# The same steps of seven interleaved lanes in other orders: a two-layer graph-attention and feed-forward kernel

## The chip, the cores and the metric

The kernel runs on one core of one Trainium2 chip. The time is device microseconds of one launch, from its first to its last instruction and what the runtime adds; lower is better. In the text PE is the matmul engine (PEld its weight loads), DVE the vector engine, ACT the scalar engine, POOL the GpSimd engine and SP the engine that issues most DMAs.

## The reference

The input is x, 64 batches of 256 tokens with 256 numbers each, in float32, and an adjacency matrix of 256 x 256. Two layers follow each other; every stage starts with a layer norm and is added to x.

```python
x = x + gnn0(layernorm(x), adj)     # mlp1, attention over all tokens, mlp2, attention over adj
x = x + ffn0(layernorm(x))          # the top half of the tokens by a score goes through gelu MLP
x = x + gnn1(layernorm(x), adj)     # one attention layer over adj
x = x + ffn1(layernorm(x))          # Mamba-2 block: conv, 8 heads of decays, gated norm, projection
```

ffn0 has to know the rank of every token within its batch (a token's score against all 256), gathers the upper half in the order of rank, and scatters the result back. Batches are independent of each other.

## The kernel before, in words

Two batches form a group of 4 x 128 tokens, so there are 32 groups (numbered 0 to 31). Each group passes through four pieces of code, and each piece is a Python generator: it issues some instructions and yields. A piece in progress is called a lane, and it has a letter:

| letter | what it runs | steps in a group |
|---|---|---|
| a | gnn0 of a group (group 0 in two halves: a and d) | 55 (half: 42) |
| g | ranks of the tokens, scatter to DRAM, fetch of the upper half (`ranked_tokens`) | 9 |
| b | ffn0 without the ranks, and gnn1 | 50 |
| c | ffn1 (the last group in two halves: e and f) | 87 (half: 78) |
| w | weights made ready | 13, once |

Three strings say in which order the lanes take their steps. Each letter runs one step of its lane. FIRST (310 letters) starts the kernel. Then ORDER (201 letters) is repeated 29 times; each pass takes one whole group's worth of steps of every one of a, b, c and g, but of different groups: when a pass starts, a is about to begin group k, g group k-1, b has done 23 steps of k-2 and c 7 steps of k-3. An upper-case letter in ORDER allows a lane to begin its next group. LAST (407 letters) ends it. There is no scheduler beside this: the order in which instructions are issued is the order in which they stand in each engine's own queue, and an engine never overtakes in its queue. So a letter's place decides, on each of the five queues, what stands ahead of its instructions. Semaphores between engines follow from the data and the buffers.

In the text a step is named by lane and number: c8 is the eighth step of lane c. These are the steps that matter here, with the lines of the profile (all matmuls go through the helper `mm`, L239, and all transposes through `tr`, L242, so PE's rows are told apart by their tiles):

- a3: xn, the layer norm (DVE, L395). a4, a5: its transposes pt (PE), copied to xT by ACT (L409). a10 to a13, a18 to a21: matmuls pp with W_fc. a14: fb (PE), most and top (DVE, L427, L428). a15 to a17: e and its sums on DVE and ACT, then e is scaled on POOL (L470). a22, a23: transposes pt of e (PE), copied by ACT (L486). a24, a27, a30, a33: matmuls u, each followed by two exponentials on ACT (L493, L496) with DVE between and after (L495, L498), and an add on POOL (L567). a36, a37: mlp2. a38 to a41: matmuls with W_hand. a42 to a47: the second attention; a48, a51: u again. a54, a55: transposes pr, and DVE's L595 and L596.
- g2, g3: xn and score (DVE, L395, L604, L607). g5: wrow, the score along a row (PE). g6, g7: ranks (DVE, L623, L626), `to` and `back` (L632, L633). g8: four indirect DMAs from POOL that write `sorted` to DRAM (L637). g9: two DMAs on SP that fetch `taken` (L643).
- b2: psel, the transposes of `taken` (PE), copied to sel by ACT (L657). b3, b8, b13, b18: matmuls ph; after each come ACT (L673, L678), POOL (L679), DVE (L681), ACT (L682) and DVE (L684), which makes g. b23 to b30: py with g. b31: y (DVE) and its DMA to DRAM. b32: gather by POOL (L709). b33, b34: L716 on DVE, L719 on POOL, statistics L383. b39: fb. b42: e on POOL; b43, b44: its transposes. b45 to b49: pa and u. b50: statistics for c.
- c3: xn. c4, c5: transposes of xn, xT; c5 also has pd, the matmul for dt. c6: L787, L789 on DVE, Exp and Ln on ACT (L790, L791). c7: L793, L794 and the scan csT (L795) on DVE. c8: pn, transposes of dtT and csT. c10 to c30: five convolutions, each pp on PE, L857 on ACT, three L861 on DVE, Tanh on ACT (L866), L867 on DVE, with the decays E on POOL (L835) and ACT (L842) between. c33, c35, c37, c39: transposes of xs. c43, c44, c53, c54, c63, c64, c69, c70: E times cb (DVE, L915). c45, c55, c65, c71: pz; c47, c57, c67, c73: py with E; then DVE's L940 and POOL's L941. c75 to c79: the norm. c80 to c86: po.

The step function and its loops:

```python
    with tc.manual_schedule():
        for lane in FIRST:
            step(lane, True)
        while at["a"] < n:
            for letter in ORDER:
                step(letter.lower(), letter.isupper())
        for lane in LAST:
            step(lane, True)
```

Of the kernel before, what the change touches and what calls it, by code (L numbers as in the profile page):

```python
# [19 lines left out]
GELU_C = 0.7978845608028654  # L20
GELU_A = 0.044715
FIRST = (
    "dwadadaddwadwaaaaddddddadaadaddaawaaadaddadaaddaddaadaaaadadaddaawadaadadaddawddcadadaacaaadaddadaaa"
    "gwaawgggggagaaaagaawaaagaaaaaababbababagaaaaabbbbabbabbababaabababwwbaaaabababaaaabaaabbbbbabbbabaga"
    "gagbababaababbaaaaabaaggabgabbggaaabaaabagabcbbabababbbacabbaabbbbbabaaccaabcbaacawaabwbbaacbcababaa"
    "babaabgabb"
)
ORDER = (
    "cbAbcccaaccbbbbcbabacccccacccccaaaccbcbccaaaabacbcbabaaaaccbacaabcabccbccbccacaccaaGcbbaacacccbcbgcg"
    "ccacgaaacggabccccccgcccgcgbacbccccccaccbcaacBabacaabcaccbaccbbbbbcabccbccbCaaacaabacccbbacbacbbbbabb"  # L30
    "b"
)
LAST = (
    "cfefbcfcfcbfbeeefgcfeccbfcbbffebecececbcccccegeccefccbfcefebecfbcfccccccebcefbccfcebccccfcfcbccbecff"
    "bfeccbcfeccfbegffccecbbccebcceeececeececfcccbcgecffebfffeebfcfccccegfffcbccgefbgccbffbcebbfecfccbcfc"
    "cbbegffbcecbccbcgcebbefcccfcfbefccfcecbebcecececfebecfcecbfccegcfbbbcccfbecbcecbcceecfccfcefceeccfec"
    "febfebffbeccefbcbecbecfbcfebcfeccfffbcefccbbccccbfbccfbbeccbfccbcbcecefcfbceccccccccbcbfeebcbcbcbfec"
    "bcbccec"
)


# [1061 lines left out]
```

## Time and profile before

| what | value |
|---|---|
| median of 3 runs | 3633.09 us (3630.11 to 3633.62) |
| the profiled execution, its own time | 3634.4 us |
| its span in the profile | 3632.7 us |
| FIRST, by the trace | 0 to 217.0 us |
| 29 passes of ORDER | 217.0 to 3362.6 us |
| LAST | 3362.6 to 3632.7 us |
| mean granted clock of PE | 0.987 |

The bounds of the parts are the starts of the first matmuls of each part. In the profile's rows, a group is named by line, engine, operation and tiles (out<-in), with its count; "idle before" is the time that the engine stood still ahead of it, with the engine or DMA whose signal ended that. In an answer on waits the columns are the total of us, the number of times and the longest. In a row of the timeline the first two numbers are start and length in us, "xN" the number of merged instructions, and in brackets the idle time before it and what ended it. A matmul of float32 has two records in the trace, a transpose one; matmuls overlap, so their lengths add up to more than the time that they take. The runs shown lie within 0.1% of each other; the profiled execution is 1.3 us above their median.

### The profile page before, as it was taken

The numbers are of one execution on the slowest core, as the hardware profiler recorded it, in microseconds if no ns is written. First come the engines' busy times: TensorE is split into PE (matmuls) and PEld (weight loads), VectorE is DVE, ScalarE is ACT, GpSimd is POOL, SyncE is SP. The second block draws the span as 40 slices with busy tenths as digits, with TensorE's granted clock in tenths as the row PEclk, the third lists the DMA queues.
The fourth block names the chain that finished last, engine by engine and source line by source line (L and its number), as shares of the span: only waits on it lengthen the run. The fifth ranks groups of instructions, "written<-read, shape, count | busy, mean of one in ns | idle before, by whom it ended". The sixth has DMA issues, their size and how long they took to land.

```text
span 3632.7 us, 51434 instructions
## 1 busy us (share of the span) xinstructions
PE 3461.4 (95%) x16236; PEld 2445.3 (67%) x16236; DVE 2803.0 (77%) x7142; ACT 2190.2 (60%) x5166; POOL 1599.5 (44%) x2040
## 2 busy tenths in 40 slices
PE   8999999999999999999999999999999999999675
PEld 6666676676676676676676677676677676677444
DVE  5577778877788877788877787877787887787765
ACT  4466666666666666666666666666666666666443
POOL 2334444444445444444444444434444444444432
PEclk9999999999999999999999999999999999999887
DMA  3012101111201211201111211111211111211111
GB/s 116 25 45 65 62 28 60 60 63 57 65 29 57 63 60 57 66 32 52 63 60 58 66 39 50 62 57 58 66 52 38 60 58 58 66 51 34 59 53 43
DMA packets 120992, 201.29 MB, mean 55 GB/s; under 512 B 18448, under 2 KB 79760, under 8 KB 120720
## 3 DMA queue, kind: packets, MB, share of 16 engines
q1 hardware_dynamic: 108432, 164.44, 14.0%
q0 software_dynamic: 12288, 33.57, 3.0%
q8 instruction: 129, 2.11, 0.2%
q14 instruction: 143, 1.17, 0.1%
HBM read 151.03 MB, written 42.73 MB: 53 GB/s over the span
## 4 chain that ended last, share of the span: by engine, by line
PE 47%; DVE 28%; ACT 14%; POOL 5%; issue 4%; DMA 1%; SPq 0%; ACTq 0%; DVEq 0%; POOLq 0%
PE pp L239 9%; DVE xs L861 9%; PE u L239 9%; PE po L239 6%; PE py L239 5%; PE pz L239 4%; PE ph L239 4%; ACT E L842 4%; POOL e L470 3%; PE pa L239 3%; PE pt L242 3%; DVE xn L395 3%; DVE junk L729 2%; DVE st L383 2%; ACT xs L857 2%
## 5 line engine op out<-in xcount | busy, mean ns | idle before, releaser
L239 PE MATMUL pp<-W_fc,o 128*128 128x256 f32 (+1 forms) x2048 | 459.9, 379 | 0.2 <-DVE W_fc L274 0.2
L842 ACT ACTIVATE E<-E,ncs 128x256 f32<-128x256 f32 (+1 forms) x1024 | 376.8, 442 | 131.0 <-POOL E L835 131.0
L861 DVE SCALAR_TENSOR_TENSOR xs<-pp,conv_w,xs 128x510 f32<-128x510 f32 (+5 forms) x495 | 360.8, 730 | 121.5 <-ACT xs L857 92.0
L239 PEld LDWEIGHTS pp<-W_fc,o 128*128 128x128 f32 x2048 | 383.3, 190 | 67.4 <-issue 12.8
L470 POOL TENSOR_SCALAR e<-e,den 128x256 f32<-128x256 f32 x384 | 225.4, 604 | 351.8 <-DVE den L467 171.5
L239 PE MATMUL pp<-xT,W_in 128*128 128x512 f32 (+1 forms) x660 | 298.8, 586 | 0.0
L567 POOL TENSOR_TENSOR o<-w,o 128x512 f32<-128x512 f32 (+1 forms) x132 | 170.4, 1293 | 241.6 <-DVE w L498 241.6
L835 POOL TENSOR_SCALAR_AFFINE_SELECT E<-E 128x256 f32<-128x256 f32 x512 | 225.4, 470 | 104.2 <-DMA E<-csd 102.7
L915 DVE TENSOR_TENSOR E<-E,cb 128x768 f32<-128x768 f32 (+1 forms) x264 | 254.7, 996 | 0.0
L239 PE MATMUL pz<-xT,W_in 128*128 128x512 f32 (+1 forms) x528 | 248.8, 595 | 0.0
L239 PE MATMUL py<-w,g 128*128 128x256 f32 x1024 | 243.4, 385 | 5.6 <-DVE g L684 3.5
L383 DVE BATCH_NORM_STATS2 st<-xt 128x6 f32<-128x256 f32 x512 | 185.3, 414 | 79.9 <-POOL xt L764 52.4
L239 PE MATMUL ph<-sel,w 128*128 128x256 f32 x1024 | 242.5, 380 | 0.7 <-ACT sel L657 0.7
L239 PE MATMUL u<-at,h 128*128 128x256 f32 x1024 | 241.1, 384 | 0.2 <-ACT at L486 0.2
L239 PE MATMUL pp<-o,mlp_w 128*128 128x512 f32 (+1 forms) x528 | 231.2, 580 | 2.3 <-POOL o L567 2.2
L239 PE MATMUL po<-W_ol,xs 128*128 128x256 f32 x1024 | 232.7, 381 | 0.0
L239 PE MATMUL pp<-xT,mlp_w 128*128 128x512 f32 (+1 forms) x528 | 231.9, 583 | 0.2 <-ACT xT L409 0.2
L496 ACT ACTIVATE w<-w,neg 128x512 f32<-128x512 f32 (+1 forms) x196 | 139.9, 714 | 152.2 <-DVE w L495 152.1
L679 POOL TENSOR_SCALAR g<-g 128x512 f32<-128x512 f32 x128 | 91.5, 715 | 316.8 <-ACT g L678 312.0
L395 DVE TENSOR_SCALAR xn<-xt,mv,rstd 128x256 f32<-128x256 f32 x512 | 222.7, 491 | 5.6 <-POOL rstd L255 4.9
L866 ACT ACTIVATE th<-xs 128x512 f32<-128x512 f32 (+1 forms) x165 | 102.1, 619 | 207.2 <-DVE xs L861 202.9
L239 PEld LDWEIGHTS py<-w,g 128*128 128x128 f32 x1024 | 187.0, 190 | 55.3 <-DVE g L684 30.0
(174 smaller groups left out, 7906.2 us busy)
## 6 DMA issues: line engine op xcount, KB each, us to landing
E<-csd SPq DMA_DIRECT2D x248, 384.0 KB
xt<-in_x_dram SPq DMA_DIRECT2D x31, 512.0 KB
out_dram<-xt SPq DMA_DIRECT2D x31, 512.0 KB
taken<-sorted SPq DMA_DIRECT2D x64, 128.0 KB
ranked<-y SPq DMA_DIRECT2D x64, 128.0 KB
cs<-xs SPq DMA_DIRECT2D x64, 64.0 KB
E<-csd SPq DMA_DIRECT2D x16, 192.0 KB
w<-in_L_ffn_w_dram SPq DMA_DIRECT2D x2, 1024.0 KB
```

The lines of the kernel that those rows point to most:

```text
L239: nc.tensor.matmul(to, lhsT, rhs, start=start, stop=stop)
L242: nc.tensor.transpose(to, of, eye)
L383: nc.vector.bn_stats(st[:, c, :], xt[:, c, :])
L395: nc.vector.tensor_scalar(chunk(xn, c), xt[:, c, :], mv[:, c, 0:1], rstd[:, c : c + 1], ALU.subtract, ALU.mult)
L470: nc.gpsimd.tensor_scalar(e, e, den[:, c : c + 1], 1.0, ALU.mult, ALU.mult)
L496: nc.scalar.activation(w, w, AF.Exp, bias=neg1)
L567: nc.gpsimd.tensor_tensor(o1[m], w, o1[m], ALU.add)
L835: nc.gpsimd.affine_select(out=diag[:, b], in_=diag[:, b], compare_op=ALU.is_ge, fill=-3e38, base=0, pattern=[[0, 2], [1, P]], channel_mult ...
L842: nc.scalar.activation(e[:, b, to], e[:, b, to], AF.Exp, bias=ncs[:, b, half, h : h + 1])
L861: nc.vector.scalar_tensor_tensor(s3[:, :, d:], p3[:, :, : N - d], conv_w[:, m, 3 - d : 4 - d], s3[:, :, d:], ALU.mult, ALU.add)
L866: nc.scalar.activation(th, s, AF.Tanh)
L915: nc.vector.tensor_tensor(e2, e2, cb2, ALU.mult)
```

## The change

The three strings are replaced by others. Each has as many letters as before, and as many of each letter, and after FIRST and after every pass each lane stands at the same step as before. No instruction is added, removed or altered; what differs is their order in the engines' queues, and with it which buffers are in use at a time. The words given with it: "Other orders of the lanes' steps, searched in a model with longer hand-overs between engines; nothing else differs". In FIRST 85% of the letters' steps stand at another place (by 4.6 places on average), in ORDER 76% (2.4; at most 12), in LAST 97% (10.4; the steps of g up to 101 places earlier).

```diff
 FIRST = (
-    "dwadadaddwadwaaaaddddddadaadaddaawaaadaddadaaddaddaadaaaadadaddaawadaadadaddawddcadadaacaaadaddadaaa"
-    "gwaawgggggagaaaagaawaaagaaaaaababbababagaaaaabbbbabbabbababaabababwwbaaaabababaaaabaaabbbbbabbbabaga"
-    "gagbababaababbaaaaabaaggabgabbggaaabaaabagabcbbabababbbacabbaabbbbbabaaccaabcbaacawaabwbbaacbcababaa"
-    "babaabgabb"
+    "dwaaddaaddddaadwaadddadaaacdaadaadwacdwdaaaddddaadadaaaaadadddaddaaadadaaddaddadwadaadaaaadddadaagcg"
+    "aaagwgaggaagaaagaaaaawaawgaaabaabaaaaaabbaabgabbawbbbaaaabaabwbaabbabaaabbabbabababaagbabbbbabbabaaa"
+    "agagaaabagabbbbababaaaaabbaaaggbabaaabbgagagawbbaabbabaaagbbcacbacbbbaacabaabbbbabbbawcbbccaabbbaaba"
+    "baawbaaabb"
 )
 ORDER = (
-    "cbAbcccaaccbbbbcbabacccccacccccaaaccbcbccaaaabacbcbabaaaaccbacaabcabccbccbccacaccaaGcbbaacacccbcbgcg"
-    "ccacgaaacggabccccccgcccgcgbacbccccccaccbcaacBabacaabcaccbaccbbbbbcabccbccbCaaacaabacccbbacbacbbbbabb"
-    "b"
+    "bAcbcccaaccbbbcbaacbccbccacccccaaacccbbccbacaaaabbaacbcccaccbaacaaabacbabaccccbcGaaaccacabbccacaacbb"
+    "gccaccgcbagcccgacgbgcccccgaccccccagbcccccaacbBabacbbaccabaccbcccbcbbabcbcCacbbcbbacaaacabcabbbacbabb"
+    "b"
 )
 LAST = (
-    "cfefbcfcfcbfbeeefgcfeccbfcbbffebecececbcccccegeccefccbfcefebecfbcfccccccebcefbccfcebccccfcfcbccbecff"
-    "bfeccbcfeccfbegffccecbbccebcceeececeececfcccbcgecffebfffeebfcfccccegfffcbccgefbgccbffbcebbfecfccbcfc"
-    "cbbegffbcecbccbcgcebbefcccfcfbefccfcecbebcecececfebecfcecbfccegcfbbbcccfbecbcecbcceecfccfcefceeccfec"
-    "febfebffbeccefbcbecbecfbcfebcfeccfffbcefccbbccccbfbccfbbeccbfccbcbcecefcfbceccccccccbcbfeebcbcbcbfec"
-    "bcbccec"
+    "fcccbceececccbfeeefbbbccfbebfgfcgcbfeecegecefgbfcfccecfcfebecbcccffccbcccbfcccfcefbfcfcffccccefbcccc"
+    "ccbcfefcfcfccegbecccfbcceccgccbeggccecceefceffcbcefcbbegceeceebcfbbefcebeccbfccecfccbefecbcccfecebfb"
+    "cffcfcbcbfecebbccfbbbccbfecccfcbffcceceebcbebcceccecceceeefccecbcccbbcffceccgeccecbeebecceebfbebfccf"
+    "fffcfcbfebfecfcebbcbefbccbcccccbfebfffcfcfcecbcccccbbbfffbbecbccbfcfbceccebccccfbbfcefeebbbcbfcefceb"
+    "ccccefc"
 )
```

A letter whose lane cannot begin yet does nothing: so it is for 3 of c and 2 of g in FIRST, before and after, and in LAST for nearly all of e and f (and before for 10 of b). What is then left is taken in turns, a step of each lane that is left, after the string is over: before, b of the last group from step 41, c from step 85, and e and f; after, c from step 85, and e and f. In the new ORDER c8 and b25 open the pass instead of b25 and c9; c33 stands behind a14; c5 directly behind a51; b24 ahead of the next pass's c8; g5 to g8 about c57 to c65.

## The prediction

> **What bounds the kernel now.** I read the page first, then busy time by stage, then the waits of PE, then the order of time at the places where PE waits.
>
> ```profile
> span 3632.7 us, 51434 instructions
> PE 3461.4 (95%) x16236; PEld 2445.3 (67%) x16236; DVE 2803.0 (77%) x7142; ACT 2190.2 (60%) x5166; POOL 1599.5 (44%) x2040
> PEclk9999999999999999999999999999999999999887
> ```
>
> PE is the busiest engine, and its clock is whole except in the last three slices. The windows of the three parts of the schedule (FIRST, the 29 passes of ORDER, LAST; after the width come the busy times of PE, PEld, DVE, ACT and POOL with their instructions, the clock, the DMA share and GB/s):
>
> ```profile
> 0.00:217.00 217.00, 193.88 (x836) 144.63 (x836) 119.58 (x407) 111.41 (x279) 68.34 (x97) 0.98 0.19 60
> 217.00:3362.60 3145.60, 3086.40 (x14618) 2181.00 (x14618) 2505.67 (x6346) 1968.11 (x4641) 1441.23 (x1825) 1.00 0.17 55
> 3362.60:3632.70 270.10, 181.10 (x784) 119.71 (x784) 177.76 (x391) 110.65 (x249) 89.97 (x118) 0.83 0.16 52
> ```
>
> The passes hold 87% of the time, 3145.6 / 29 = 108.5 us each, and PE (first number after the width) is busy in 98% of it: any order can win back only PE's waits there. In LAST PE is idle for 89 us, but that part waits on a chain through DVE and ACT. Who PE waits for, over the whole run:
>
> ```profile
> PE pt L242 <- DVE xs L867: 40.8, 9, 7.0
> PE pt L242 <- POOL e L470: 22.3, 61, 2.7
> PE pn L242 <- DVE csT L795: 21.7, 31, 0.8
> PE pn L242 <- DVE dtT L793: 14.0, 31, 1.9
> PE pd L239 <- ACT xT L409: 7.2, 30, 0.2
> PE psel L242 <- DMA taken<-sorted: 6.7, 4, 3.3
> ```
>
> The first row (9 times) is LAST. The rows with some 30 or 60 times come in every pass. They undercount, since a matmul's end is modelled: from one matmul's start to the next, less its own length at the pace of its row, I get 3.1 us of true waiting in a pass (pn 1.4, pt of e 1.1, pd 0.4, py 0.2). That is the most the new ORDER can gain: 29 x 3.1 = 90 us.
>
> **The change, part by part.** Nothing is added or removed; 76% of ORDER's letters stand elsewhere, by 2.4 places on average. So I take each place where PE waits, or nearly waits, and compare the matmuls that cover the wait with the chain that has to end in it. Starts of matmuls are 0.216 us apart for 256 columns, 0.43 for 512, 0.109 for a transpose, and a pass takes about 4% more than their sum.
>
> *1. The ranks (g5 to b2).* The chain today:
>
> ```profile
> 1906.88 0.60 PE L242 MATMUL wrow<-ident,wc 128*128 128x128 f32 x4
> 1914.32 0.45 DVE L632 CAST to<-rank 128x4 uint32<-128x4 f32 x1
> 1915.28 1.63 POOL L637 DMA_INDIRECT sorted<-xn,to  x1 [0.18 <-issue]
> 1922.59 0.97 POOL L637 DMA_INDIRECT sorted<-xn,to  x1 [1.72 <-DMA sorted<-xn,to]
> 1921.07 4.45 SPq L643 DMA_DIRECT2D taken<-sorted  x2
> DMA to landing us min/median/max: 2.4/2.5/3.7
> 1928.64 0.60 PE L242 MATMUL psel<-ident,taken 128*128 128x128 f32 x4
> ```
>
> From the end of `to` (1914.8) to the landing of `taken` is 0.5 + 8.3 of POOL + 1.6 to the second issue on SP (0.32 long, over at 1925.5) + 2.5 = 12.9 us, all latency that no order shortens. PE asks for it 13.8 us after `to`: under 1 us to spare, and 4 passes already waited. In the new order the work of PE between wrow and psel falls from 20.1 us to 17.95 (a36 and c65 and much else change sides), by today's ratio (21.3 real) to 19.0. DVE needs after wrow: about 1.1 until gz and xs of c56 and c58 are out of its way, then g6 2.0, b48 1.1, g7 2.6, in all 7.0. So PE arrives 12.0 us after `to`: a wait of 0.9 to 1.2 us. I take **+1.2**, as POOL also has c59, b48 and c61 ahead of the scatter.
>
> *2. pd (c5).* Each pass xT's copy ends just before pd. In the new order a51's matmuls stand directly before c5, so on ACT the exponential of a51 (0.60 us) stands ahead of that copy and cannot start until a51 ends. The wait goes from 0.4 to about 0.05 + 0.3 + 0.6 + 0.6 - 0.43 = 1.2: **+0.8**. Behind that copy on ACT stand a52, b16 and c6.
>
> *3. pn (c8).*
>
> ```profile
> 1949.80 1.11 PE L239 MATMUL pd<-xT,W_dt 128*32 128x256 f32 x8 [0.24 <-ACT xT L409]
> 1954.90 0.31 PE L242 MATMUL pn<-ident,dtT 64*128 64x64 f32 x2 [0.37 <-DVE dtT L793]
> 1955.90 0.33 PE L242 MATMUL pn<-ident,csT 64*128 64x64 f32 x2 [0.70 <-DVE csT L795]
> 1956.17 1.13 PE L239 MATMUL py<-w,g 128*128 128x256 f32 x4
> ```
>
> From the end of pd to csT is 4.9 us. The new order puts b24's py (0.85) ahead of pn: the cover goes from 3.4 to 4.3. But a54's two operations on DVE (0.68 + 0.69) now follow b18 on PE and stand straight before c7; they push csT to 5.2. Net **-0.4**.
>
> *4. xs's transposes (c33).* They go from after a18 and a19 (3.4 us of matmul) to directly behind fb of a14, and need L867 of c30. On DVE that now stands behind b34, whose statistics wait for POOL's add:
>
> ```profile
> 1876.41 0.74 DVE L383 BATCH_NORM_STATS2 st<-xt 128x6 f32<-128x256 f32 x2
> 1877.88 0.75 DVE L383 BATCH_NORM_STATS2 st<-xt 128x6 f32<-128x256 f32 x2 [0.72 <-POOL xt L719]
> 1878.55 0.36 DVE L385 BATCH_NORM_AGGREGATE mv<-st 128x2 f32<-128x6 f32 x4
> ```
>
> b34 ends at 1878.9, L867 takes 0.69: 1879.6, and PE would be at c33 at 1878.1 to 1878.6. **+1.0**. In return c35 and c33 are out of the way of a22, whose e (L470) waits for the same DVE queue: the two waits of a22 and a23 nearly go, **-0.9**.
>
> *5. Smaller ones.* a4 comes one py (0.88) earlier against xn of a3, which had 0.95 to spare with DVE 0.4 sooner: +0.5. b26 meets g of b22 half a microsecond sooner: +0.3. c4 waits for c3, now behind b11 and b12 on DVE: +0.3. The next pass's b13 and b18, po (c80 to c86), pa and the E products of c63, c64, c69, c70 keep 0.5 us or more and are costed at nothing; if DVE runs a microsecond late, py of c47, c57 and c67 is late next.
>
> *6. Credit.* While PE waits, DVE, ACT and POOL go on, so a later wait is shorter: -0.7, an estimate: a quarter of the sum of items 1 to 5 (1.2 + 0.8 - 0.4 + 1.0 - 0.9 + 1.1 = 2.8). I round the remainder to **+2.0 us a pass**, 58 us in 29.
>
> *The clock.* Windows with the same columns:
>
> ```profile
> 123.00:126.40 3.40, 1.71 (x9) 1.00 (x10) 0.57 (x2) 1.30 (x5) 1.86 (x4) 0.99 0.02 5
> 126.40:129.80 3.40, 3.40 (x10) 2.69 (x9) 0.69 (x1) 1.11 (x2) 0.62 (x1) 0.50 0.00 0
> ```
>
> PE was idle for half of one stretch (one wait, 2.9 us), and the next ran at 0.50. The Trainium skill ("TensorE: Matmul & The Clock Gate", Part 1: The HAM clock gate) asks for at least one idle window of about 3.4 us before the clock halves; by it my waits would never cost more than themselves. The row says less is enough. Waits up to 1.9 us left the clock whole (psel's of 1.1 us at 1601, 224.6 with 1.9). By page and row alike the sum stays at +58 with waits of 1.2; but by the row a psel wait of 2.5 us would add half of 3.4, 1.7 us a pass, 49 us.
>
> *FIRST and LAST.* FIRST: the 2.9 us wait for e at 124 and the two around 45 keep their neighbours; 0, between -5 and +5. LAST: the last group's ranks (g) come up to 101 places sooner. Today PE waits 2.30 + 3.26 us there for `taken`, and then runs at half clock for a while. The wait goes; c30 starts some 5 us sooner and b31's `y` some 9 sooner, of which DVE takes back 3 to 6, since b33 now stands on DVE ahead of c56 and waits through the gather with nothing beside it. The tail of e and f, taken in turns, stays. **-6**, between -12 and +8.
>
> *Sum.* 3634.4 (the profiled execution's own time; span 3632.7) + 58 - 6 = 3686. The median shown is 1.3 lower, so 3685.
>
> **The rivals.**
> - *Faster.* If item 1 does not bite, because DVE reaches g7 a microsecond sooner (b48 or c58 in its shadow), and c30's L867 is out before fb, then what is left is what the new order covers better: pn (4.3 instead of 3.4), a22, a51. Waits would fall from 3.1 to some 1.5 us a pass: -46 - 6, 3582; half of it gives 3608. It decides where `to` ends: 13 us before psel. For it: three of the five repeated waits get more cover. Against: the hand-overs in these rows are 0.05 to 0.1 us, so an order chosen for long ones buys cover that this chip does not need.
> - *No change.* Gains and losses in a pass cancel, and LAST gives its 6: 3628. The letters are locally permuted, and PE is busy 98%; but that needs a cancellation within 0.25 us a pass.
> - *Much slower.* The wait for `taken` passes 2.5 us and the clock halves once a pass: 3685 + 38 (a further 1.3 us a pass) or more, 3723 to 3740. For it: POOL's queue ahead of the scatter; against: c61 is ready early.
> - *That it does not do what it says*: each string keeps its count of each letter, so after FIRST and every pass each lane stands at the same step; the change is order alone.
>
> **How the numbers follow.** Some 0.2% (7 us) is what a measurement of this kernel can tell. Slower as worked out, 3650 to 3723: 0.59. Much slower: 0.15. Within 7 us: 0.06. Faster: 0.20. Predicted 3685. The range goes down to 3605, which leaves about 0.12 of the faster case out, and up to 3740 with 0.06 beyond.
>
> **What would show it.** Right: a pass of about 110.5 instead of 108.5; PE's wait of psel for `taken` in most passes, some 1 us each; pd's idle up from 0.24; pt of xs (L867) waiting in every pass; pn's wait for dtT gone. Wrong: psel without waits, or a pass under 108.5. If the clock shows 0.5 inside the passes, the third rival is at work.

## The result, and the profile after

| | before | after |
|---|---|---|
| median | 3632.89 us (3630.11 to 3633.62, 4 runs) | 3712.95 us (3709.76 to 3719.19, 4 runs) |
| profiled execution, its own time | 3634.4 us | 3710.0 us |
| FIRST | 217.0 us | 217.3 us |
| 29 passes of ORDER | 3145.6 us (108.5 each) | 3221.3 us (111.1 each) |
| LAST | 270.1 us | 269.7 us |

The changed kernel is slower: ratio 1.0224, 95% interval 1.0206 to 1.0242, so 80 us. The three parts of the schedule, as busy time by stage with the columns of before:

```profile
0.00:217.30 217.30, 192.90 (x836) 144.94 (x837) 121.12 (x407) 112.44 (x281) 68.12 (x98) 0.98 0.21 63
217.30:3438.60 3221.30, 3123.32 (x14618) 2204.31 (x14617) 2547.78 (x6347) 1964.78 (x4641) 1477.66 (x1826) 0.99 0.17 54
3438.60:3708.30 269.70, 178.26 (x784) 119.25 (x784) 171.75 (x390) 107.47 (x244) 87.40 (x117) 0.82 0.16 52
```

Of the 75.6 us between the two profiled executions the passes hold 75.7, FIRST 0.3 and LAST -0.4. Two things in the row of the passes are odd for a mere change of order: DVE is busy 42 us longer (2547.78 against 2505.67) and PE 37 us, with the same instructions, and PE's clock is 0.99 instead of 1.00. Waits of PE over the whole run:

```profile
PE pt L242 <- DVE xs L867: 59.6, 38, 8.9
PE pd L239 <- ACT xT L409: 55.3, 31, 1.8
PE pn L242 <- DVE csT L795: 20.1, 32, 0.8
PE pt L242 <- POOL e L470: 7.6, 5, 2.9
PE pn L242 <- DVE dtT L793: 6.9, 4, 2.2
PE psel L242 <- DMA taken<-sorted: 2.2, 3, 1.2
```

pd's wait for xT has grown from 7.2 to 55.3 us, once in every pass. This is the place in the order of time; the first pd in the list is k = 0, the second has to wait for the second copy of xT:

```profile
1091.60 0.60 ACT L493 ACTIVATE w<-u 128x512 f32<-128x512 f32 x1 [0.23 <-PE u L239]
1092.16 2.35 POOL L770 TENSOR_TENSOR xt<-xt,b_lin 128x1024 f32<-128x1024 f32 x1
1092.23 2.56 DVE L495 TENSOR_SCALAR w<-w 128x512 f32<-128x512 f32 x1 [1.12 <-ACT w L493]
1094.10 0.62 PE L239 MATMUL pd<-xT,W_dt 128*32 128x256 f32 x4
1094.83 0.72 ACT L496 ACTIVATE w<-w,neg 128x512 f32<-128x512 f32 x1 [2.15 <-DVE w L495]
1095.46 0.58 ACT L493 ACTIVATE w<-u 128x512 f32<-128x512 f32 x1
1095.93 0.58 ACT L409 COPY xT<-pt 128x512 f32<-128x512 f32 x1
1096.56 0.63 PE L239 MATMUL pd<-xT,W_dt 128*32 128x256 f32 x4 [1.84 <-ACT xT L409]
1097.12 3.05 PE L239 MATMUL ph<-sel,w 128*128 128x256 f32 x8
```

L495, a minimum over 128x512 that takes 0.42 us elsewhere, takes 2.56 us here. It starts 0.07 us after POOL's L770, the add of b_lin in c5, and ends 0.28 us after that add ends. ACT's L496 waits for it (2.15 us), the next exponential and the copy of xT stand behind L496, and PE at pd. In the kernel before the same add begins beside other operations:

```profile
1948.78 2.36 POOL L770 TENSOR_TENSOR xt<-xt,b_lin 128x1024 f32<-128x1024 f32 x1 [5.73 <-DVE xn L395]
1948.84 0.69 DVE L498 SCALAR_TENSOR_TENSOR w<-w,u 128x512 f32<-128x512 f32 x1
1950.96 0.48 DVE L787 TENSOR_SCALAR dtT<-pd,dtb 64x256 f32<-64x256 f32 x1 [1.43 <-PE pd L239]
```

L498 runs within the add and is not longer for it. So theory A is: L495 stands still while the add runs, and that is the whole loss. Its rival (B) is the prediction's own account of pd, the exponential of a51 ahead of the copy on ACT.

The last line of the fence of the kernel after shows a second effect: eight matmuls ph took 3.05 us instead of some 1.9. The clock halves. Four stretches of 3.41 us, in two pairs that follow each other (after the width PE, PEld, DVE, ACT and POOL, then the clock, the DMA share and GB/s):

```profile
1094.46:1097.88 3.42, 1.58 (x12) 0.83 (x9) 2.57 (x6) 2.92 (x5) 0.05 (x1) 1.00 0.00 0
1097.88:1101.29 3.41, 3.41 (x13) 2.85 (x12) 1.71 (x4) 2.97 (x7) 0.00 (x0) 0.50 0.02 5
```

```profile
1207.10:1210.52 3.42, 1.80 (x10) 1.26 (x11) 2.71 (x6) 2.97 (x6) 0.00 (x0) 1.00 0.02 5
1210.52:1213.93 3.41, 3.41 (x22) 2.80 (x20) 3.08 (x7) 3.29 (x6) 0.00 (x0) 1.00 0.00 0
```

The same wait at pd lies in both pairs. Where PE was busy 1.58 us of the stretch, the next ran at 0.50; where it was busy 1.80, nothing happened. (Experiment 5 shows that this share alone does not decide it.) All the stretches of half clock in the passes begin on one grid of 3.413 us, and 14 of the 29 passes have one, as a rule where the wait falls into a single stretch of the grid. From one wrow to the next (28 of these, which leave out the ends), passes without one take 110.04 us on average and passes with one 112.15.

### The profile page after: what moved, and what is told of

Same layout as the page of the kernel before. It is cut to its first block, busy times and chain, and to the rows that moved or that the text cites. A ratio compares the mean times of both kernels' runs of the same rounds, so it can differ in the third digit from the quotient of the medians.

```text
span 3708.3 us, 51267 instructions
## 1 busy us (share of the span) xinstructions
PE 3494.5 (94%) x16236; PEld 2468.5 (67%) x16236; DVE 2840.6 (77%) x7142; ACT 2184.7 (59%) x5166; POOL 1633.2 (44%) x2040
## 3 DMA queue, kind: packets, MB, share of 16 engines
q1 hardware_dynamic: 108432, 164.44, 13.6%
q8 instruction: 129, 2.11, 0.2%
## 4 chain that ended last, share of the span: by engine, by line
PE 44%; DVE 34%; ACT 9%; POOL 6%; issue 5%; DMA 1%; SPq 0%; POOLq 0%; ACTq 0%; DVEq 0%
DVE xs L861 9%; PE pp L239 9%; PE ph L239 6%; PE u L239 6%; PE po L239 6%; PE py L239 5%; PE pz L239 4%; ACT E L842 4%; DVE junk L729 3%; PE pa L239 3%; DVE xn L395 3%; DVE w L495 2%; POOL e L470 2%; DVE e L451 2%; DVE xd L881 2%
## 5 line engine op out<-in xcount | busy, mean ns | idle before, releaser
L470 POOL TENSOR_SCALAR e<-e,den 128x256 f32<-128x256 f32 x384 | 267.1, 710 | 391.5 <-DVE den L467 195.9
L239 PE MATMUL ph<-sel,w 128*128 128x256 f32 x1024 | 267.2, 407 | 0.0
L239 PE MATMUL u<-at,h 128*128 128x256 f32 x1024 | 249.7, 388 | 0.0
L915 DVE TENSOR_TENSOR E<-E,cb 128x768 f32<-128x768 f32 (+1 forms) x264 | 244.9, 960 | 0.3 <-issue 0.2
L239 PEld LDWEIGHTS ph<-sel,w 128*128 128x128 f32 x1024 | 198.2, 201 | 64.2 <-ACT sel L657 24.5
L383 DVE BATCH_NORM_STATS2 st<-xt 128x6 f32<-128x256 f32 x512 | 185.2, 414 | 64.6 <-POOL xt L764 37.5
L496 ACT ACTIVATE w<-w,neg 128x512 f32<-128x512 f32 (+1 forms) x196 | 138.8, 709 | 148.4 <-DVE w L495 144.5
```

Source lines behind the costliest of these rows:

```text
L239: nc.tensor.matmul(to, lhsT, rhs, start=start, stop=stop)
L383: nc.vector.bn_stats(st[:, c, :], xt[:, c, :])
L470: nc.gpsimd.tensor_scalar(e, e, den[:, c : c + 1], 1.0, ALU.mult, ALU.mult)
L496: nc.scalar.activation(w, w, AF.Exp, bias=neg1)
L915: nc.vector.tensor_tensor(e2, e2, cb2, ALU.mult)
```

## The experiments

All ratios are to the kernel before, measured beside it on the same chip. That kernel's median was 3634 us for experiments 1 to 3, 3642 for 5 to 7 and 3639 for 4 and 8, so ratios are compared, not times.

**1. Where the loss lies: the new ORDER alone.**

```diff
 FIRST = (unchanged)
-ORDER = ("cbAbcccaaccbbbbcbab...
+ORDER = ("bAcbcccaaccbbbcbaac...
 LAST = (unchanged)
```

> The kernel before with the new ORDER, its own FIRST and LAST. By the trace the 29 passes took 3221.3 us in the changed kernel and 3145.6 before, FIRST and LAST 0.3 more and 0.4 less. Theory (the whole loss lies in the passes): 3633 + 76 = 3709, within 8 us of the changed kernel. Rival (the new FIRST and LAST gain or lose something that the passes hide, by leaving buffers in another state): more than 10 us away from it.

3711.78 us, ratio 1.0220 (1.0203 to 1.0237), against 1.0224 for the whole change. L495 is 2.6 us long in 29 places, and 14 stretches of half clock lie in the passes. ORDER carries all of it; FIRST and LAST together are worth nothing that can be told.

**2. Taking the add away, in both orders.**

```diff
-            nc.gpsimd.tensor_tensor(xt, xt, b_lin.unsqueeze(1).to_broadcast([P, C, D]), ALU.add)
```

> The changed kernel without L770, POOL's add of b_lin to xt in c5 (the output lacks b_lin). Theory A (DVE's L495 in a50 takes 2.56 us instead of 0.43 because it starts 0.07 us after that 2.35 us add and stands still until the add is over; ACT's exponential L496 and xT's copy wait behind it, and PE at pd; the 2.0 us wait then halves the clock in 15 passes): L495 is 0.43 long there, pd waits 0.4 to 1.2 us, no clock of 0.5 within the passes, time 3713 - 29 x (0.8 to 1.6) - 15 x 1.4 = 3646 to 3669. Theory B (the exponential of a51 ahead of xT's copy on ACT is what delays pd, as the prediction had it): pd still waits 2.0, time within 10 us of 3713.

> The control: the kernel before without L770 (the output lacks b_lin). There the add lies beside L498 and L787, neither of which is longer for it. Both theories: 3633, within 5 us; a gain of 10 us or more would say that the add costs something in any order.

The changed kernel without the add: 3632.78 us, ratio 0.9998 (0.9989 to 1.0007). The kernel before without it: 3631.55 us, 0.9993 (0.9985 to 1.0002). So an add that costs nothing in the old order costs the whole 80 us in the new one. Two of PE's waits in the changed kernel without the add:

```profile
PE pt L242 <- DVE xs L866: 59.1, 38, 8.9
PE pd L239 <- ACT xT L409: 6.9, 31, 1.3
```

pd is back to 6.9 us (7.2 before the change), and there is no half clock in the passes. A pass takes 108.44 us from wrow to wrow, against 108.45 before the change. The gain is larger than the 3646 to 3669 expected, for two reasons: pd's wait falls to 0.34 us and not to 0.4 to 1.2, no more than the 0.40 of before, so the exponential ahead of the copy costs nothing (B falls); and a stretch of half clock had cost 2.1 us and not 1.4.

**3. A smaller dose: the add in two halves.**

```diff
-            nc.gpsimd.tensor_tensor(xt, xt, b_lin.unsqueeze(1).to_broadcast([P, C, D]), ALU.add)
+            for half in (slice(0, C // 2), slice(C // 2, C)):
+                nc.gpsimd.tensor_tensor(xt[:, half], xt[:, half], b_lin.unsqueeze(1).to_broadcast([P, C // 2, D]), ALU.add)
```

> The changed kernel with L770 as two adds of 128x512 (about 1.2 us each) instead of one of 128x1024. Theory A: L495 waits for the first half alone, so it is 1.4 us long instead of 2.56, pd waits 0.8 to 1.0 us instead of 2.0, the clock stays whole in the passes: 3713 - 29 x 1.1 - 21 = 3660. If POOL's second half also goes ahead of L495: 3713. Theory B: 3713.

3652.15 us, ratio 1.0048 (1.0031 to 1.0065), somewhat better than the 3660 expected, since a stretch of half clock had cost more than was put in. In order of time, L771 being the add with its two halves merged in one row:

```profile
1082.90 2.68 POOL L771 TENSOR_TENSOR xt<-xt,b_lin 128x512 f32<-128x512 f32 x2
1082.97 1.48 DVE L495 TENSOR_SCALAR w<-w 128x512 f32<-128x512 f32 x1 [1.12 <-ACT w L493]
1086.22 0.63 PE L239 MATMUL pd<-xT,W_dt 128*32 128x256 f32 x4 [0.75 <-ACT xT L409]
```

L495 stands still for the first half alone: it is over at 1084.45, while the second half runs from 1084.13 to 1085.58. No stretch of half clock is left in the passes. The three doses in a row, each from its trace (waits from one matmul's start to the next):

| add | L495 | pd's wait, us a pass | passes with half clock | us a pass |
|---|---|---|---|---|
| whole | 2.56 | 2.01 | 14 of 29 | 111.0 |
| two halves | 1.48 | 0.92 | none | 109.06 |
| none | 0.42 | 0.34 | none | 108.44 |

From none to halves the pass grows by 0.62 and the wait by 0.58. From none to whole the wait grows by 1.67, and the passes at whole clock (110.04) by 1.60.

**4. What of L495 makes it stand still: another form of it.** In the fence of the kernel before, in the section on the result, L498 was not held. It reads one operand from SBUF, the memory of this kernel's tiles, and one from PSUM, where its matmuls put their results. So L495 gets that form, with the same result (beside the add in the kernel before lie L498 and L787; L684, which the expectation names too, does not):

```diff
-            nc.vector.tensor_scalar(w, w, 1.0, None, ALU.min)
+            nc.vector.scalar_tensor_tensor(w, w, 1.0, u, ALU.min, ALU.bypass)
```

> The changed kernel, order and add untouched, with another form of L495: scalar_tensor_tensor(w, w, 1.0, u, min, bypass), whose second operand lies in PSUM, instead of tensor_scalar(w, w, 1.0, None, min); the result is the same. Theory A1 (L495 stands still because this form streams SBUF through a port that POOL's add holds, as the Trainium skill's page SBUF - State Buffer says of such forms; L498 and L684, which lay beside the add in the kernel before, were not longer): L495 about 0.69 us everywhere, not over 1; pd waits 0.5 to 0.9 us; no clock of 0.5 in the passes; 3713 - 29 x (1.1 to 1.5) - 20 = 3650 to 3661. Theory A2 (any operation of DVE on SBUF that meets the add stands still): 2.6 us again, 3713 or more.

> The control for after_min_stt: the kernel before with that form of L495. DVE works 0.27 us more at each of 188 places, 51 us in all, with DVE 77% busy and off the path: 3633 to 3645. Above that, the longer form itself costs time and after_min_stt has to be read against this run.

The changed kernel with it: 3634.12 us, ratio 0.9987 (0.9979 to 0.9994), with order, add and computation whole. That is 16 us better than the 3650 to 3661 expected: pd's wait fell to the 0.34 us of experiment 2, not to 0.5 to 0.9, and no stretch of half clock is left in the passes.

```profile
1835.14 2.36 POOL L770 TENSOR_TENSOR xt<-xt,b_lin 128x1024 f32<-128x1024 f32 x1
1835.21 0.69 DVE L495 SCALAR_TENSOR_TENSOR w<-w,u 128x512 f32<-128x512 f32 x1 [1.11 <-ACT w L493]
1837.88 0.62 PE L239 MATMUL pd<-xT,W_dt 128*32 128x256 f32 x4 [0.17 <-ACT xT L409]
```

At the same 0.07 us behind the add, L495 now takes 0.69 us. A1 holds and A2 falls. That agrees with the Trainium skill ("SBUF — State Buffer", Who interferes with whom): a tensor_scalar on float32 in SBUF can use a second pair of ports that it shares with GpSimd, and whoever holds the pair keeps the other out for its whole instruction; an operation with one input in SBUF and outside that mode does not need it. The trace shows the standstill and its end with the add; that it is a port, only the page says. The gain of 0.13% is less than the 0.2% that can be told of this kernel.

The operation's name is not what decides. L793 is a scalar_tensor_tensor as well, but with both inputs in SBUF. In the kernel before one of them, in LAST, began 0.56 us after an L770 (3448.51, 2.36 us long) and was over 0.29 us after its end; its median is 0.41 us. What the operations held here have in common is that all they read lay in SBUF, though that alone is not enough: the statistics L383, which read SBUF too, kept their 0.41 us in the changed kernel in all 64 records that begin within an add on POOL. L793:

```profile
3449.07 2.09 DVE L793 SCALAR_TENSOR_TENSOR dtT<-dtT,dz 64x256 f32<-64x256 f32 x1 [2.21 <-ACT dz L791]
```

The control missed. The kernel before with this form: 3669.46 us, ratio 1.0079 (1.0062 to 1.0096), where 0 to 12 us were expected. A pass takes 1.5 us more in the profiled execution, which is 11 us above the median. psel waits 14 times instead of 4:

```profile
PE psel L242 <- DMA taken<-sorted: 19.3, 14, 3.2
```

"Off the path" was the error, since two of DVE's longer L495s stand close ahead of the ranks in its queue. One pass with such a wait, in order of time:

```profile
1821.46 0.60 PE L242 MATMUL wrow<-ident,wc 128*128 128x128 f32 x4
1830.04 0.17 DVE L632 CAST to<-rank 128x4 uint32<-128x4 f32 x1
1840.83 0.97 POOL L637 DMA_INDIRECT sorted<-xn,to  x1 [2.75 <-DMA sorted<-xn,to]
1841.60 3.01 DVE L762 TENSOR_SCALAR w<-w 128x512 f32<-128x512 f32 x1
1841.83 1.27 POOL L764 TENSOR_TENSOR xt<-w,xt 128x512 f32<-128x512 f32 x1
1843.06 1.26 POOL L941 TENSOR_TENSOR xs<-xs,gz 128x512 f32<-128x512 f32 x1
1845.32 0.55 PE L242 MATMUL psel<-ident,taken 128*128 128x128 f32 x3 [1.54 <-DMA taken<-sorted]
```

`to` ends 8.75 us after wrow here, and 9.03 in most passes, where it was 7.89 before. So psel follows `to` by 13.1 to 13.3 us instead of 13.9, beside the 12.9 that its chain needs, and a late scatter is enough to make PE wait. L762 shows the same standstill as L495: it began during POOL's L637 and was over only after the two operations that followed it, and in all 13 cases over 0.8 us it began while POOL was at work. But psel does not wait for it: in this order it stands behind g9 and begins 11 us after `to`, and one pass waited 1.1 us at psel with L762 at 0.62. psel's longer waits make 0.5 of the 1.5 us that a pass grew by, and those of pt for xn some 0.4, in every pass. The rest, and why the scatter was late in some passes, was not traced further, so the cost of this form in the old order is not settled.

**5. A better place for the add?** By the trace POOL was free in c12 and DVE worked on PSUM.

```diff
-            nc.gpsimd.tensor_tensor(xt, xt, b_lin.unsqueeze(1).to_broadcast([P, C, D]), ALU.add)
 ... (from c5 to c12)
+                if m == KI:
+                    nc.gpsimd.tensor_tensor(xt, xt, b_lin.unsqueeze(1).to_broadcast([P, C, D]), ALU.add)
                 th = columns("m", "th")
```

> The changed kernel with L770 issued in c12 instead of c5, where by the trace POOL is free and DVE works on PSUM (L861); the computation is whole. Theory A (where the add lies is all that costs): as without it, 3633, or up to 3 us more for the decays L835 behind it on POOL. Rival (the add costs about as much wherever it lies, because some operation of DVE meets it): L495 whole again, but another of DVE's (L818 or xn, L395) about 2 us long and a pass of over 109.5: 3660 or more.

3702.68 us, ratio 1.0168 (1.0155 to 1.0182): the rival was right.

```profile
1334.08 2.46 POOL L865 TENSOR_TENSOR xt<-xt,b_lin 128x1024 f32<-128x1024 f32 x1
1334.47 2.11 DVE L816 TENSOR_SCALAR ncs<-ccs 128x32 f32<-128x32 f32 x1
1338.71 1.59 DVE L395 TENSOR_SCALAR xn<-xt,mv,rstd 128x256 f32<-128x256 f32 x4
1339.17 1.95 PE L242 MATMUL pt<-ident,xn 128*128 128x128 f32 x8 [1.07 <-DVE xn L395]
```

The operation that is caught is now L816, 32 columns wide: it takes 2.11 us instead of 0.18 and is over as the add ends, while two copies out of PSUM (L811, the same 32 columns) that began within the add kept their 0.18 us. Behind L816 the convolution and xn are late, and PE waits at a4 and a5 (2.1 us a pass). The length of the victim doesn't matter; its moment and its form do.

Nine stretches of half clock lie in these passes. One of them, with the stretch ahead of it:

```profile
2223.09:2226.50 3.41, 2.17 (x12) 1.30 (x11) 3.38 (x8) 1.84 (x4) 1.59 (x4) 1.00 0.97 375
2226.50:2229.92 3.42, 3.42 (x7) 1.82 (x6) 2.59 (x5) 2.00 (x6) 0.00 (x0) 0.50 0.00 1
```

PE was busy 2.17 us here, more than the 1.80 that left the clock whole in the changed kernel; 1.74 of the 2.17 are the transposes of a4 and a5. The stretch from 1892.0 has 2.18 and was followed by a whole clock. Whether a transpose counts like a matmul for the clock was not tested.

**6. Two more exchanges of letters**, on top of 5: a18 ahead of c33 (so that the transposes of xs come later), then also c7 ahead of a54.

```diff
-  c32 c33 c34 a17 c35 c36 b38 a18 a19 c37
+  c32 a17 b38 a18 c33 c34 a19 c35 c36 c37
```

```diff
-  a54 c7
+  c7 a54
```

> As after_add_c12, and in ORDER a17, b38 and a18 ahead of c33 and c34 (so that a18's matmuls stand between fb of a14 and the transposes of xs), a19 behind them. Theory (c33 behind fb costs its measured wait): the wait of pt for xs (L867), 0.66 us a pass, goes, and that for e (0.77) stays since the same matmuls stand ahead of a22: 3633 - 29 x 0.66 = 3614. Rival (the later c33 holds up DVE's L881 and with it e): 3633, within 4 us.

> As after_add_c12_a18, and c7 ahead of a54 in ORDER, so that DVE's L793 to L795 stand ahead of a54's L595 and L596. Theory: csT comes some 0.5 us sooner and pn's wait for it falls from 0.67 to about 0.15 us a pass: 3614 - 29 x 0.5 = 3600. Rival (DVE then waits for Ln with nothing beside it, and what follows on it, a55 and g of b22, is late): 3614, within 4 us, with py waiting for g.

Ratios 1.0175 (1.0162 to 1.0189) and 1.0213 (1.0199 to 1.0227), against 1.0168 for experiment 5: nothing gained, then a loss. The expected times were worked from 3633, which experiment 5 had not reached; the differences can be read still. With a18 first, pt's waits for xs (L867, here L868) and for e, from experiment 5 to this one:

```profile
PE pt L242 <- DVE xs L868: 60.4, 29, 8.9
PE pt L242 <- POOL e L470: 7.4, 7, 2.9
```

```profile
PE pt L242 <- DVE xs L868: 46.8, 9, 8.9
PE pt L242 <- POOL e L470: 28.4, 35, 2.9
```

xs waits 13.6 us less (what is left lies in LAST), and e 21 us more. With c7 first pn's wait went, and py's wait for g (L684) rose to 39.2 us. Both rivals named the place: the time came back at the next wait, and in the second case more than was won.

**7. One pair alone, in the old order: b24 ahead of c8.**

```diff
-    "cbAbcccaaccbbbbcbab...
+    "bcAbcccaaccbbbbcbab...
```

> The kernel before with one pair of letters exchanged at the head of ORDER: b24 (0.85 us of py) ahead of c8 (pn), as in the new order. Nothing else of the new order. Theory (the cover of csT is worth what the waits of pn were): pn waits 0.37 + 0.70 us a pass before, and would wait 0.2; a pass falls from 108.45 to about 107.6: 3634 - 29 x 0.85 = 3609. Rival (the time comes back at the next wait, for e in a22 or pd): 3634, within 4 us.

Ratio 0.9999 (0.9991 to 1.0008), a miss by all of the 25 us forecast. Two waits of PE:

```profile
PE py L239 <- DVE g L684: 27.9, 58, 1.8
PE pn L242 <- DVE csT L795: 8.8, 31, 0.7
```

pn's wait for dtT has gone and that for csT fell from 21.7 to 8.8, but py waits 27.9 us for g instead of 3.5: b24 came so early that its own g was not there.

**8. The last 28 steps of ORDER, crossed.** From c1 on the two orders are exchanged (b12 goes with them). The first of the two runs:

```diff
-  c1 a47 c2 b12 b13 c3 b14 b15 a48 c4 a49 a50 a51 c5 a52 b16 ...
+  c1 a47 a48 a49 c2 a50 a51 b13 a52 c3 c4 c5 b14 b15 a53 c6 ...
```

> The changed kernel with the last 28 steps of ORDER, from c1 on (and b12), in the order of before: a51 ahead of b13, c3 to c5 behind b13. Theory (the loss sits in the order of those 28 steps, where L495 and the add meet; the rest of ORDER is worth nothing): L495 whole, pd waits 0.4, 3633 within 10 us. Rival (the first 173 steps cost time too, which the tail hid): 3650 or more.

> The kernel before with those last 28 steps in the new order. Theory: L495 is 2.56 us long, pd waits 2.0 us, the clock halves in about half of the passes: 3690 to 3715. Rival (what POOL and DVE carry over from the first 173 steps decides whether the two meet, so the old head with the new tail doesn't meet): 3633 within 10 us.

New head and old tail: ratio 1.0076 (1.0059 to 1.0093). Old head and new tail: 1.0151 (1.0128 to 1.0175). The meeting goes with the tail: L495 is 2.6 us long in 29 places of the second and in none of the first. The second came out as its theory had it (3697.97 us, with 17 stretches of half clock). The first did not: the new head with the old tail loses 1.2 us a pass without any meeting in the passes. Its waits of py for g and of pt for xs were 3.5 and 40.8 us before:

```profile
PE pt L242 <- DVE xs L867: 61.7, 38, 8.9
PE py L239 <- DVE g L684: 25.2, 57, 0.7
```

The wait for xs is in the whole new order too (59.1 us without the add, with nothing lost), so py's is the new one. How the 1.2 us are made up was not traced further. In a queue that never overtakes, a stretch of the order cannot be priced apart from what it joins.

## Why the prediction was right, and where its steps were not

Slower was right and 3685 was 28 us short of 3713, but the number came out by luck of its terms: of +2.0 us a pass the largest, 1.2, was put on a step that cost nothing, and the cost that decided it was in none. By the prediction's own signs the account failed: "psel without waits" was one of being wrong, and the clock showed 0.5 inside the passes, which was the sign of the third rival. Per pass, measured from one matmul's start to the next:

| step | forecast | measured |
|---|---|---|
| 1 psel | +1.2 | 0 (3 waits in the run) |
| 2 pd | +0.8, by a51's exponential | +1.6, by L495 held in L770 |
| 3 pn | -0.4 | -0.5 |
| 4 xs / e | +1.0 / -0.9 | +0.64 / -0.33 |
| 5 smaller ones and 6 credit | +1.1, -0.7 | near 0 |
| clock | 0 | 14 of 29 passes, 2.1 us each: +1.0 |
| LAST, once | -6 | -0.4 |

- *psel.* The chain after `to` was right, its start was not. `to` ends 6.45 us after wrow, not 7.0, and psel comes 19.3 us after wrow, not 19.0:

```profile
1054.70 0.65 PE L242 MATMUL wrow<-ident,wc 128*128 128x128 f32 x4
1060.99 0.17 DVE L632 CAST to<-rank 128x4 uint32<-128x4 f32 x1
1074.00 0.60 PE L242 MATMUL psel<-ident,taken 128*128 128x128 f32 x4
```

  From the end of `to` to psel are 12.85 us, beside 12.9 that the chain needs: it arrives just in time (the second fetch is issued 10.04 us after `to`, and with the 2.5 to landing that makes 12.5). Two errors, of 0.55 and 0.3 us, made a wait of 0.9 us out of nothing, and that was taken as 1.2. That the margin is this thin, the control in experiment 4 shows.
- *pd.* The mechanism was wrong. I counted ACT's queue and forgot POOL's L770 in the same step c5, 2.36 us long, and what runs on DVE while it does. Without the add the queue on ACT costs nothing (0.34 against 0.40 us).
- *The clock.* That less than an idle stretch of 3.4 us is enough was right, and the case (the rival "much slower") was laid out, but the edge of 2.5 us was put too high, and at psel. The Trainium skill's rule ("TensorE: Matmul & The Clock Gate", Part 1: The HAM clock gate: a window without work, of 3413 ns, free-running) fits the grid seen here, but not the edge: PE was busy in 46% of the stretch that halved the clock, and in 64% in experiment 5. A wait of 2.0 us does it, as a rule, in the passes where it falls wholly into one stretch. The third rival's sum was short by the prediction's own row: 3685 + 38 has the longer wait, but not the 49 us that the halved clock was said to add.
- *No change* was nearer than its chance of 0.06: without the add the new order ties with the old one to 0.01 us a pass. Gains at pn and e and losses at xs and in small places cancel, which was luck too.
- *LAST.* psel's 5.6 us of waiting went, as forecast, but fb of b39 waits once for 14.5 us instead of 2.9, behind DVE's L716 that waits for the gather. I had counted 3 to 6 us back; it was all of it.
- *The sum.* Its small sums were loose: the terms of pd give 1.1 and not 1.2, those of pn -0.6 and not -0.4, and 2.8 less 0.7 is 2.1. What was measured adds up: 1.60 us a pass, the longer wait at pd, is 46 us in 29, and 14 half-clocked passes at 2.1 are 29: 75 of the 75.7.

## What to carry to other kernels

When an order of issue changes, price not only whether an engine's queue is longer but which operations on VectorE now run at the same time as a long GpSimd operation: a float32 tensor_scalar in SBUF was held until its end, however small it was, while a form with one input in SBUF and one in PSUM ran through. In a profile this is seen in the spread of durations of one instruction, not in its median: before the change L762 had a median of 0.42 us and a maximum of 2.35. And where an engine that is 98% busy waits at five places, moving one instruction earlier mostly moves the wait; only the chain that ends last at the next place tells whether anything is won.

## What the runs showed of the hardware that was not expected

- VectorE's tensor_scalar stood still from 0.07 us (L495) or 0.39 us (L816) after GpSimd's add began until its end: 2.56 instead of 0.42 us for 512 columns, 2.11 instead of 0.18 for 32. The scalar_tensor_tensor with one operand in PSUM took 0.69 us at the same place; one with both operands in SBUF (L793) was held, 2.09 instead of 0.41 us.
- GpSimd operations that follow each other within 0.05 us can hold it beyond the first (L762, 3.01 us, over the end of one and two more), while between the halves of the add in experiment 3 it got in. What decides that is open.
- The matmul clock halved for one stretch of 3.41 us of a fixed grid. In the changed kernel this came after stretches in which PE was busy for 1.57 or 1.58 us; 1.80 left it whole, and so did one with 1.57. In experiment 5 it came after 2.17 us as well. So the busy share that the profile shows does not give the edge, and what does is open. The halving cost 2.1 us in a pass of the changed kernel, more than half of a stretch (1.7); DVE and PE behind it were late too, but the difference was not traced.
